# Field products of embeddings: embedding depth on the partitions, the batch along the free dimension, one fixed weight, all loads in the sync queue, and two tiles loaded ahead instead of three

## Chip, cores, metric

One core of one Trainium2 chip. The metric is device time in microseconds (us) for one execution; the host's preparation of arrays is not in it. A kernel's time is the median of its runs; a profile, and every number read from it, is of one execution; "1302" for the kernel before was measured again (medians 1301.9 to 1302.3 us).

## The reference

```python
def reference(r_x, L0_rec_W):            # x: (4096, 32, 64), W: (64, 64), fp32
    vid = jnp.einsum('bfd,de->bfe', x, W)
    idx_i, idx_j = jnp.triu_indices(32, k=1)        # 496 pairs of fields
    return x[:, idx_i, :] * vid[:, idx_j, :]        # (4096, 496, 64)
```

The output has 520 MB, the input 34 MB. All arithmetic is small beside the writing.

## The kernel before

Batch rows lie on the partitions. A tile is 128 rows with all 32 fields; two tiles share one load. W multiplies from the right, so each pair of fields is transposed by TensorE first, copied out of PSUM, multiplied, and copied again; VectorE then forms the pair products into one of three output buffers, and each buffer is stored on the sync queue. Mid-run loads go on the scalar queue, three loads ahead.

```python
    R = 2                       # tiles per load
    SLOT = 171                  # pairs (of 64 elements) in an output buffer
    AHEAD = 3                   # loads ahead, and x buffers
    ...
    def load(g):
        queue = nc.sync if g < AHEAD else nc.scalar
        xt = xpool.tile([P, R, F, D], F32, tag="x", name=f"x_{g}")
        ...                     # g == 0: in three pieces
            queue.dma_start(out=xt, in_=xg[g])
    ...
    def project(xt, r, tag, order):
        for g in order:         # four groups of four pairs of fields
            for k, pair in enumerate(pairs):
                nc.tensor.transpose(pt[:, k, :], xt[:, r, 2*pair : 2*pair+2, :], ident)
            nc.scalar.copy(xT[:, g*TPB : (g+1)*TPB, :], pt)
            for k, pair in enumerate(pairs):
                for h in range(2):
                    nc.tensor.matmul(pv[:, h, k, :], lhsT=xT[h*D:(h+1)*D, pair, :],
                                     rhs=w2[h*D:(h+1)*D, :], start=True, stop=True)
            nc.scalar.copy(vid[...], pv[:, :, :TPB, :])
    ...
            nc.vector.tensor_tensor(ot[...], xt[:, r, i:i+1, :].to_broadcast([P, n, D]),
                                    vid[:, i+1:, :], ALU.mult)
    ...                         # then one store of the buffer on nc.sync
```

Of the kernel before, what the change touches and what calls it, by code (L numbers as in the profile page):

```python
# [1 line left out]

# [5 lines left out]

F32 = mybir.dt.float32
ALU = mybir.AluOpType  # L10



SLOTS = [(0, 6), (6, 13), (13, 31)]

FIRST = [(13, 31, [24, 18, 13]), (6, 13, [10, 8, 6]), (0, 6, [4, 2, 0])]
SECOND = [(0, 6, [2, 4, 6]), (6, 13, [8, 10, 13]), (13, 31, [18, 31])]


@with_exitstack  # L20
def pairwise_bilinear_kernel(
    ctx: ExitStack,
    tc: tile.TileContext,
    x: bass.AP,
    w: bass.AP,
    out: bass.AP,
):
    nc = tc.nc
    P = 128
    B, F, D = x.shape  # L30
    NP = F * (F - 1) // 2

    R = 2
    G = B // (P * R)


    TPB = 4
    GRP = F // 2 // TPB
    SLOT = 171
    AHEAD = 3  # L40

    xg = x.rearrange("(g p r) f d -> g p r f d", p=P, r=R)
    og = out.rearrange("(g p r) n d -> g p r n d", p=P, r=R)
    off = [i * (F - 1) - i * (i - 1) // 2 for i in range(F)]

    const = ctx.enter_context(tc.tile_pool(name="const", bufs=1))
    xpool = ctx.enter_context(tc.tile_pool(name="x", bufs=AHEAD))
    tpool = ctx.enter_context(tc.tile_pool(name="xT", bufs=1))
    vpool = ctx.enter_context(tc.tile_pool(name="vid", bufs=2))
    opool = ctx.enter_context(tc.tile_pool(name="out", bufs=3))  # L50
    ps_t = ctx.enter_context(
        tc.tile_pool(name="ps_t", bufs=4, space=bass.MemoryType.PSUM)
    )
    ps_v = ctx.enter_context(
        tc.tile_pool(name="ps_v", bufs=2, space=bass.MemoryType.PSUM)
    )

    w2 = const.tile([P, D], F32)
    nc.scalar.dma_start(out=w2[0:D, :], in_=w)
    nc.scalar.dma_start(out=w2[D : 2 * D, :], in_=w)  # L60

    def load(g):
        queue = nc.sync if g < AHEAD else nc.scalar
        xt = xpool.tile([P, R, F, D], F32, tag="x", name=f"x_{g}")
        if g == 0:
            h = F // 2
            nc.sync.dma_start(out=xt[:, 0, h:, :], in_=xg[g][:, 0, h:, :])
            nc.sync.dma_start(out=xt[:, 0, :h, :], in_=xg[g][:, 0, :h, :])
            for r in range(1, R):
                nc.sync.dma_start(out=xt[:, r], in_=xg[g][:, r])  # L70
        else:
            queue.dma_start(out=xt, in_=xg[g])
        return xt

    loaded = [load(g) for g in range(AHEAD)]

    ident = const.tile([P, P], F32)
    make_identity(nc, ident)

    def project(xt, r, tag, order):  # L80

        xT = tpool.tile([P, F // 2, P], F32, tag="xT", name=f"xT_{tag}")
        vid = vpool.tile([P, F // 2, 2, D], F32, tag="vid", name=f"vid_{tag}")
        for g in order:
            pairs = range(g * TPB, (g + 1) * TPB)
            pt = ps_t.tile([P, TPB, P], F32, tag="pt", name=f"pt_{tag}_{g}")
            for k, pair in enumerate(pairs):
                nc.tensor.transpose(  # L88
                    pt[:, k, :], xt[:, r, 2 * pair : 2 * pair + 2, :], ident
                )  # L90
            nc.scalar.copy(xT[:, g * TPB : (g + 1) * TPB, :], pt)  # L91

            pv = ps_v.tile([P, 2, 2 * TPB, D], F32, tag="pv", name=f"pv_{tag}_{g}")
            for k, pair in enumerate(pairs):
                for h in range(2):
                    nc.tensor.matmul(  # L96
                        pv[:, h, k, :],
                        lhsT=xT[h * D : (h + 1) * D, pair, :],
                        rhs=w2[h * D : (h + 1) * D, :],
                        start=True,  # L100
                        stop=True,
                    )
            nc.scalar.copy(  # L103
                vid[:, g * TPB : (g + 1) * TPB].rearrange("p k h e -> p h k e"),
                pv[:, :, :TPB, :],
            )
        return vid.rearrange("p g h e -> p (g h) e")

    def products(xt, vid, ot, base, r, fields):
        for i in fields:  # L110
            n = F - 1 - i
            nc.vector.tensor_tensor(  # L112
                ot[:, off[i] - base : off[i] - base + n, :],
                xt[:, r, i : i + 1, :].to_broadcast([P, n, D]),
                vid[:, i + 1 :, :],
                ALU.mult,
            )

    for g in range(G):
        xt = loaded[g]  # L120
        for r in range(R):
            t = g * R + r
            first = t == 0
            vid = project(xt, r, t, range(GRP - 1, -1, -1) if first else range(GRP))
            plan = FIRST if first else SECOND if t == 1 else None
            for s, (lo, hi) in enumerate(SLOTS):
                if plan:
                    lo, hi, ends = plan[s]
                else:
                    ends = [hi]  # L130
                ot = opool.tile([P, SLOT, D], F32, tag="o", name=f"o_{t}_{s}")
                base = off[lo]
                at = hi if first else lo
                for e in ends:
                    a, b = (e, at) if first else (at, e)
                    products(xt, vid, ot, base, r, range(b - 1, a - 1, -1) if first else range(a, b))
                    nc.sync.dma_start(
                        out=og[g][:, r, off[a] : off[b], :],
                        in_=ot[:, off[a] - base : off[b] - base, :],
                    )  # L140
                    at = e
        if g + AHEAD < G:
            loaded.append(load(g + AHEAD))


_INS = ["r_x", "L0_rec_W"]
_OUTS = [((4096, 496, 64), "float32")]


# [21 lines left out]
```

## Time and profile before

| | before |
|---|---|
| time | 1301.97 us (1301.0 to 1302.68) |
| span of the profiled run | 1300.3 us |
| written, read | 520.09 MB, 33.59 MB |
| VectorE, TensorE, ScalarE busy | 87%, 26%, 10% of the span |
| share of 16 DMA engines, sync and scalar queue | 94.5% and 4.9% |

The page is to be read for what fills the span. The compute engines do not; the DMA queues do. What is left to find in such a kernel is where the sixteen DMA engines are *not* moving data, and that needs the rate by stretches of time. The prediction below shows those lines.

The last 26.8 us of the span show how evenly the engines run dry (columns: stretch, length, busy us of TensorE, its weight loads, VectorE, ScalarE, GpSimd with counts, granted TensorE clock, DMA share, GB/s). The kernel before:

```profile
1273.50:1300.30 26.80, 0.00 (x0) 0.00 (x0) 0.64 (x4) 0.00 (x0) 0.00 (x0) 0.50 0.69 296
```

Computing is over here but for 0.64 us and the stores are queued, yet the engines are busy for only 69% of the stretch: some have finished while others still have stores to do.

### The profile page before, as it was taken

The numbers are of one execution on the slowest core, as the hardware profiler recorded it, in microseconds if no ns is written. First come the engines' busy times: TensorE is split into PE (matmuls) and PEld (weight loads), VectorE is DVE, ScalarE is ACT, GpSimd is POOL, SyncE is SP. The second block draws the span as 40 slices with busy tenths as digits, with TensorE's granted clock in tenths as the row PEclk, the third lists the DMA queues.
The fourth block names the chain that finished last, engine by engine and source line by source line (L and its number), as shares of the span: only waits on it lengthen the run. The fifth ranks groups of instructions, "written<-read, shape, count | busy, mean of one in ns | idle before, by whom it ended". The sixth has DMA issues, their size and how long they took to land.

```text
span 1300.3 us, 6845 instructions
## 1 busy us (share of the span) xinstructions
PE 336.3 (26%) x2560; PEld 315.8 (24%) x2560; DVE 1132.8 (87%) x992; ACT 136.4 (10%) x257; POOL 0.7 (0%) x6
## 2 busy tenths in 40 slices
PE   7333213332033320333203332033330233321000
PEld 6333203332033320333203332033330223311000
DVE  6999979889798897988979899798987979999991
ACT  3111101111011110111101111001110011110000
POOL 0000000000000000000000000000000000000000
PEclk9555555555555555555555555555555555555555
DMA  9999999999999999999999999999999999999997
GB/s 384 430 421 439 428 430 436 423 432 430 428 429 430 434 422 436 435 422 433 433 429 431 423 434 424 430 435 428 433 426 427 437 421 430 434 433 431 436 431 318
DMA packets 18193, 554.12 MB, mean 426 GB/s; under 512 B 2160, under 2 KB 2160, under 8 KB 2544
## 3 DMA queue, kind: packets, MB, share of 16 engines
q1 hardware_dynamic: 16128, 526.39, 94.5%
q10 hardware_dynamic: 2032, 27.30, 4.9%
q8 instruction: 20, 0.33, 0.1%
q14 instruction: 13, 0.11, 0.0%
HBM read 33.59 MB, written 520.09 MB: 426 GB/s over the span
## 4 chain that ended last, share of the span: by engine, by line
DMA 62%; DVE 35%; issue 1%; PE 0%; DVEq 0%; ACT 0%
DMA out_dram<-o 61%; DVE o L112 35%; DMA x<-in_r_x_dram 0%; PE pt L88 0%; PE pv L96 0%; DVEq L166 0%; DVEq L112 0%; ACT vid L103 0%
## 5 line engine op out<-in xcount | busy, mean ns | idle before, releaser
L112 DVE TENSOR_TENSOR o<-x,vid 128x64 f32<-128x64 f32 (+30 forms) x992 | 1132.8, 1219 | 141.3 <-DMA out_dram<-o 130.2
L96 PE MATMUL pv<-w,xT 64*128 64x64 f32 x2048 | 230.0, 413 | 862.0 <-ACT vid L103 827.8
L96 PEld LDWEIGHTS pv<-w,xT 64*128 64x128 f32 x2048 | 218.2, 320 | 878.6 <-ACT vid L103 837.7
L103 ACT COPY vid<-pv 128x512 f32<-128x512 f32 x128 | 72.1, 587 | 1060.2 <-DVE o L112 971.3
L88 PE MATMUL pt<-ident,x 128*128 128x128 f32 x512 | 108.8, 397 | 5.4 <-DMA x<-in_r_x_dram 5.4
L88 PEld LDWEIGHTS pt<-ident,x 128*128 128x128 f32 x512 | 97.6, 212 | 9.0 <-issue 5.3
L91 ACT COPY xT<-pt 128x512 f32<-128x512 f32 x128 | 66.4, 610 | 5.7 <-PE pt L88 5.6
L91 ACT ACT_TABLE_LOAD x1 | 1.3, 1283 | 2.0 <-issue 2.0
masks.py:199 POOL TENSOR_SCALAR_AFFINE_SELECT ident<-ident 128x128 f32<-128x128 f32 x1 | 0.3, 292 | 0.1
masks.py:197 POOL MEMSET ident<- 128x128 f32 x1 | 0.2, 204 | 0.3 <-POOLq L157 0.3
L157 POOL MEMSET const-bfloat16-1.0<- 128x1 bf16 x1 | 0.1, 102 | 0.0
L157 POOL MEMSET const-uint8-127<- 128x1 uint8 x1 | 0.1, 102 | 0.0
L157 POOL MEMSET const-float32-0.0<- 128x1 f32 x1 | 0.1, 99 | 0.2 <-issue 0.2
L157 POOL MEMSET const-float32-1.0<- 128x1 f32 x1 | 0.1, 99 | 0.0
## 6 DMA issues: line engine op xcount, KB each, us to landing
out_dram<-o SPq DMA_DIRECT2D x60, 5472.0 KB, 25.5
out_dram<-o SPq DMA_DIRECT2D x30, 4928.0 KB, 28.4
x<-in_r_x_dram ACTq DMA_DIRECT2D x13, 2048.0 KB, 23.0
out_dram<-o SPq DMA_DIRECT2D x2, 2560.0 KB, 12.8
x<-in_r_x_dram SPq DMA_DIRECT2D x2, 2048.0 KB, 14.4
out_dram<-o SPq DMA_DIRECT2D x2, 1952.0 KB, 11.6
out_dram<-o SPq DMA_DIRECT2D x2, 1920.0 KB, 11.6
out_dram<-o SPq DMA_DIRECT2D x2, 1824.0 KB, 11.6
```

Source lines behind the costliest of these rows:

```text
L88: nc.tensor.transpose(pt[:, k, :], xt[:, r, 2 * pair : 2 * pair + 2, :], ident)
L91: nc.scalar.copy(xT[:, g * TPB : (g + 1) * TPB, :], pt)
L96: nc.tensor.matmul(pv[:, h, k, :], lhsT=xT[h * D : (h + 1) * D, pair, :], rhs=w2[h * D : (h + 1) * D, :], start=True, stop=True,)
L103: nc.scalar.copy(vid[:, g * TPB : (g + 1) * TPB].rearrange("p k h e -> p h k e"), pv[:, :, :TPB, :],)
L112: nc.vector.tensor_tensor(ot[:, off[i] - base : off[i] - base + n, :], xt[:, r, i : i + 1, :].to_broadcast([P, n, D]), vid[:, i + 1 :, :], ...
L157: nc = _bacc.Bacc("TRN2", target_bir_lowering=False, num_devices=1)
```

## The change

The host permutes x to (tile, 2 x 64 depth, field, 128 batch rows), so the depth that the product contracts is already on the partitions. W becomes the stationary operand of every matmul, and transposes, the identity and one of the two PSUM copies go. Instructions become twice as wide and fewer. The output is written in the same order and permuted back by the host. At the same time the loads move to the sync queue, in program order among the stores, and only two tiles are loaded ahead (4.2 MB instead of 6.3; the x tile is still 16 KB a partition).

Two words are used from here on. A *ring* is the part of a queue that one DMA engine works off. A *seam* is a load that stands among stores, with the change from stores to the load and back.

```diff
-    SLOT = 171
-    AHEAD = 3
+    SLOT = 83                     # pairs of 128 elements
+    AHEAD = 2
...
-        queue = nc.sync if g < AHEAD else nc.scalar
-        xt = xpool.tile([P, R, F, D], F32, tag="x", name=f"x_{g}")
+            xs[t] = xpool.tile([P, F, C], F32, tag="x", name=f"x_{t}")
+        nc.sync.dma_start(out=xs[t][:, lo:hi, :], in_=x[t][:, lo:hi, :])
...
-                nc.tensor.transpose(pt[:, k, :], xt[:, r, 2*pair : 2*pair+2, :], ident)
-            nc.scalar.copy(xT[:, g * TPB : (g + 1) * TPB, :], pt)
...
-                        pv[:, h, k, :],
-                        lhsT=xT[h * D : (h + 1) * D, pair, :],
-                        rhs=w2[h * D : (h + 1) * D, :],
+                        pv[half, b : b + BANK, :],
+                        lhsT=w2[half, :],
+                        rhs=xs[t][half, f : f + BANK, :],
...
+                store(t, ot, base, base, top)
+                if 1 <= n <= PIECES and t + 1 < NT and t + 1 not in (0, 1):
+                    load(t + 1, (n - 1) * F // PIECES, n * F // PIECES)
...
+    x = x.reshape(2, NT, C, F, D).transpose(1, 0, 4, 3, 2).reshape(NT, 2 * D, F, C)
```

More of the change, by code (lines that the diff above doesn't have):

```diff
@@ L5 @@
 from concourse import mybir
-from concourse.masks import make_identity
 from concourse._compat import with_exitstack
@@ L10 @@
 ALU = mybir.AluOpType
-SLOTS = [(0, 6), (6, 13), (13, 31)]
-FIRST = [(13, 31, [24, 18, 13]), (6, 13, [10, 8, 6]), (0, 6, [4, 2, 0])]
-SECOND = [(0, 6, [2, 4, 6]), (6, 13, [8, 10, 13]), (13, 31, [18, 31])]
+P = 128
+C = 128
 @with_exitstack
@@ L28, in pairwise_bilinear_kernel @@
     nc = tc.nc
-    P = 128
-    B, F, D = x.shape
+    NT, _, F, _ = x.shape
+    D = P // 2
     NP = F * (F - 1) // 2
-    R = 2
-    G = B // (P * R)
-    TPB = 4
-    GRP = F // 2 // TPB
-    SLOT = 171
-    AHEAD = 3
-    xg = x.rearrange("(g p r) f d -> g p r f d", p=P, r=R)
-    og = out.rearrange("(g p r) n d -> g p r n d", p=P, r=R)
+    GRP = 8
+    NGRP = F // GRP
+    BANK = 512 // C
+    SLOT = 83
+    AHEAD = 2
+    PIECES = 1
     off = [i * (F - 1) - i * (i - 1) // 2 for i in range(F)]
+    ctx.enter_context(tc.manual_schedule(engines={mybir.EngineType.SP}))
     const = ctx.enter_context(tc.tile_pool(name="const", bufs=1))
     xpool = ctx.enter_context(tc.tile_pool(name="x", bufs=AHEAD))
-    tpool = ctx.enter_context(tc.tile_pool(name="xT", bufs=1))
     vpool = ctx.enter_context(tc.tile_pool(name="vid", bufs=2))
     opool = ctx.enter_context(tc.tile_pool(name="out", bufs=3))
-    ps_t = ctx.enter_context(
-        tc.tile_pool(name="ps_t", bufs=4, space=bass.MemoryType.PSUM)
-    )
-    ps_v = ctx.enter_context(
-        tc.tile_pool(name="ps_v", bufs=2, space=bass.MemoryType.PSUM)
+    psum = ctx.enter_context(
+        tc.tile_pool(name="ps", bufs=4, space=bass.MemoryType.PSUM)
     )
@@ L60, in pairwise_bilinear_kernel, with load, project @@
     nc.scalar.dma_start(out=w2[D : 2 * D, :], in_=w)
-    def load(g):
-        queue = nc.sync if g < AHEAD else nc.scalar
-        xt = xpool.tile([P, R, F, D], F32, tag="x", name=f"x_{g}")
-        if g == 0:
-            h = F // 2
-            nc.sync.dma_start(out=xt[:, 0, h:, :], in_=xg[g][:, 0, h:, :])
-            nc.sync.dma_start(out=xt[:, 0, :h, :], in_=xg[g][:, 0, :h, :])
-            for r in range(1, R):
-                nc.sync.dma_start(out=xt[:, r], in_=xg[g][:, r])
-        else:
-            queue.dma_start(out=xt, in_=xg[g])
-        return xt
-    loaded = [load(g) for g in range(AHEAD)]
-    ident = const.tile([P, P], F32)
-    make_identity(nc, ident)
-    def project(xt, r, tag, order):
-        xT = tpool.tile([P, F // 2, P], F32, tag="xT", name=f"xT_{tag}")
-        vid = vpool.tile([P, F // 2, 2, D], F32, tag="vid", name=f"vid_{tag}")
-        for g in order:
-            pairs = range(g * TPB, (g + 1) * TPB)
-            pt = ps_t.tile([P, TPB, P], F32, tag="pt", name=f"pt_{tag}_{g}")
-            for k, pair in enumerate(pairs):
-                nc.tensor.transpose(
-                    pt[:, k, :], xt[:, r, 2 * pair : 2 * pair + 2, :], ident
-                )
-            nc.scalar.copy(xT[:, g * TPB : (g + 1) * TPB, :], pt)
-            pv = ps_v.tile([P, 2, 2 * TPB, D], F32, tag="pv", name=f"pv_{tag}_{g}")
-            for k, pair in enumerate(pairs):
+    xs = {}
+    def load(t, lo, hi):
+        if t not in xs:
+            xs[t] = xpool.tile([P, F, C], F32, tag="x", name=f"x_{t}")
+        nc.sync.dma_start(out=xs[t][:, lo:hi, :], in_=x[t][:, lo:hi, :])
+    def project(t, order):
+        vid = vpool.tile([P, F, C], F32, tag="vid", name=f"vid_{t}")
+        for g in order:
+            pv = psum.tile([P, GRP, C], F32, tag="pv", name=f"pv_{t}_{g}")
+            for b in range(0, GRP, BANK):
+                f = g * GRP + b
                 for h in range(2):
+                    half = slice(h * D, (h + 1) * D)
                     nc.tensor.matmul(
-                        pv[:, h, k, :],
-                        lhsT=xT[h * D : (h + 1) * D, pair, :],
-                        rhs=w2[h * D : (h + 1) * D, :],
+                        pv[half, b : b + BANK, :],
+                        lhsT=w2[half, :],
+                        rhs=xs[t][half, f : f + BANK, :],
                         start=True,
@@ L102, in project, with products @@
                     )
-            nc.scalar.copy(
-                vid[:, g * TPB : (g + 1) * TPB].rearrange("p k h e -> p h k e"),
-                pv[:, :, :TPB, :],
-            )
-        return vid.rearrange("p g h e -> p (g h) e")
-    def products(xt, vid, ot, base, r, fields):
-        for i in fields:
-            n = F - 1 - i
+            nc.scalar.copy(vid[:, g * GRP : (g + 1) * GRP, :], pv)
+        return vid
+    def products(t, vid, ot, base, a, b, backwards=False):
+        fields = [i for i in range(F - 1) if off[i] < b and off[i + 1] > a]
+        for i in reversed(fields) if backwards else fields:
+            s, e = max(a, off[i]), min(b, off[i + 1])
+            j = i + 1 + s - off[i]
@@ L112, in products @@
             nc.vector.tensor_tensor(
-                ot[:, off[i] - base : off[i] - base + n, :],
-                xt[:, r, i : i + 1, :].to_broadcast([P, n, D]),
-                vid[:, i + 1 :, :],
+                ot[:, s - base : e - base, :],
+                xs[t][:, i : i + 1, :].to_broadcast([P, e - s, C]),
+                vid[:, j : j + e - s, :],
                 ALU.mult,
             )
-    for g in range(G):
-        xt = loaded[g]
-        for r in range(R):
-            t = g * R + r
-            first = t == 0
-            vid = project(xt, r, t, range(GRP - 1, -1, -1) if first else range(GRP))
-            plan = FIRST if first else SECOND if t == 1 else None
-            for s, (lo, hi) in enumerate(SLOTS):
-                if plan:
-                    lo, hi, ends = plan[s]
-                else:
-                    ends = [hi]
-                ot = opool.tile([P, SLOT, D], F32, tag="o", name=f"o_{t}_{s}")
-                base = off[lo]
-                at = hi if first else lo
-                for e in ends:
-                    a, b = (e, at) if first else (at, e)
-                    products(xt, vid, ot, base, r, range(b - 1, a - 1, -1) if first else range(a, b))
-                    nc.sync.dma_start(
-                        out=og[g][:, r, off[a] : off[b], :],
-                        in_=ot[:, off[a] - base : off[b] - base, :],
-                    )
-                    at = e
-        if g + AHEAD < G:
-            loaded.append(load(g + AHEAD))
@@ new lines, in store @@
+    def store(t, ot, base, a, b):
+        nc.sync.dma_start(out=out[t][:, a:b, :], in_=ot[:, a - base : b - base, :])
+    for g in reversed(range(NGRP)):
+        load(0, g * GRP, (g + 1) * GRP)
+    load(1, F // 2, F)
+    load(1, 0, F // 2)
+    for t in range(NT):
+        vid = project(t, reversed(range(NGRP)) if t == 0 else range(NGRP))
+        bases = list(range(0, NP, SLOT))
+        if t == 0:
+            ends = [NP, off[27], off[24], off[21], bases[-1]]
+            for n, base in enumerate(reversed(bases)):
+                top = min(base + SLOT, NP)
+                if n:
+                    ends = [top, (base + top) // 2, base]
+                ot = opool.tile([P, SLOT, C], F32, tag="o", name=f"o_{t}_{n}")
+                for b, a in zip(ends, ends[1:]):
+                    products(t, vid, ot, base, a, b, backwards=True)
+                    store(t, ot, base, a, b)
+        else:
+            for n, base in enumerate(bases):
+                top = min(base + SLOT, NP)
+                ot = opool.tile([P, SLOT, C], F32, tag="o", name=f"o_{t}_{n}")
+                products(t, vid, ot, base, base, top)
+                store(t, ot, base, base, top)
+                if 1 <= n <= PIECES and t + 1 < NT and t + 1 not in (0, 1):
+                    load(t + 1, (n - 1) * F // PIECES, n * F // PIECES)
@@ L157 @@
     nc = _bacc.Bacc("TRN2", target_bir_lowering=False, num_devices=1)
+    x = _np.asarray(inputs["r_x"])
+    B, F, D = x.shape
+    NT = B // (2 * C)
+    x = x.reshape(2, NT, C, F, D).transpose(1, 0, 4, 3, 2).reshape(NT, 2 * D, F, C)
     arrays, args = {}, []
-    for name in _INS:
-        a = _np.ascontiguousarray(inputs[name])
+    for name, a in zip(_INS, (x, inputs["L0_rec_W"])):
+        a = _np.ascontiguousarray(a)
         arrays[f"in_{name}_dram"] = a
@@ L164 @@
         dt = _mybir.dt.from_np(_np.dtype(dtype))
-        args.append(nc.dram_tensor(f"out_{i}_dram", shape, dt, kind="ExternalOutput").ap())
+        laid = (NT, 2 * D, shape[1], C)
+        args.append(nc.dram_tensor(f"out_{i}_dram", laid, dt, kind="ExternalOutput").ap())
     with _tile.TileContext(nc) as tc:
@@ L168 @@
     r = _run(nc, [arrays], core_ids=[0])
-    got = tuple(r.results[0][f"out_{i}_dram"] for i in range(len(_OUTS)))
-    return got[0]
+    got = r.results[0]["out_0_dram"].reshape(NT, 2, D, _OUTS[0][0][1], C)
+    return _np.ascontiguousarray(got.transpose(1, 0, 4, 3, 2)).reshape(_OUTS[0][0])
```

## The prediction

> **What bounds the kernel now.** I read the page from the top: busy shares, then the slices and queues, then the chain that ended last; after that the windows view for the two ends of the run, where a transfer-bound kernel can still differ.
>
> ```profile
> span 1300.3 us, 6845 instructions
> PE 336.3 (26%) x2560; PEld 315.8 (24%) x2560; DVE 1132.8 (87%) x992; ACT 136.4 (10%) x257; POOL 0.7 (0%) x6
> ...
> q1 hardware_dynamic: 16128, 526.39, 94.5%
> q10 hardware_dynamic: 2032, 27.30, 4.9%
> q8 instruction: 20, 0.33, 0.1%
> ...
> HBM read 33.59 MB, written 520.09 MB: 426 GB/s over the span
> DMA 62%; DVE 35%; issue 1%; PE 0%; DVEq 0%; ACT 0%
> ```
>
> The reader should see two things. TensorE and ScalarE, which the change relieves, are busy for 26% and 10%. The packets of the queues fill 94.5 + 4.9 = 99.4% of the sixteen DMA engines' span. VectorE's 35% of the chain misleads: it alternates with the stores because each of the three output buffers is filled, stored and filled again. The waits settle it: VectorE's 130 us of waiting are nearly all for output stores to land, and while it works on one buffer, the stores of the two others are queued. So **the store and load traffic is the bound**, from a few us after the start to the end. The windows view says where it falls short of full rate (columns: stretch, length, busy of each engine with counts, granted TensorE clock, DMA share, GB/s):
>
> ```profile
> 0.00:3.00 3.00, 0.00 (x0) 0.00 (x0) 0.00 (x0) 1.03 (x1) 0.70 (x6) 1.00 0.34 94
> 3.00:6.00 3.00, 0.64 (x3) 0.67 (x4) 0.00 (x0) 0.25 (x1) 0.00 (x0) 1.00 0.97 341
> 6.00:15.00 9.00, 9.00 (x67) 8.55 (x66) 3.85 (x10) 3.96 (x7) 0.00 (x0) 1.00 1.03 438
> 15.00:20.00 5.00, 4.85 (x50) 4.21 (x50) 5.00 (x6) 2.41 (x6) 0.00 (x0) 1.00 0.98 372
> ...
> 100.00:1280.00 1180.00, 291.71 (x2176) 274.33 (x2176) 1043.97 (x920) 115.71 (x220) 0.00 (x0) 0.53 1.00 430
> 1280.00:1300.30 20.30, 0.00 (x0) 0.00 (x0) 0.00 (x0) 0.00 (x0) 0.00 (x0) 0.50 0.58 252
> ```
>
> The time can be put together from this. 554.12 MB at the 430 GB/s of the middle is 1288.7 us. The start loses 3 x (1 - 94/430) + 3 x (1 - 341/430) + 5 x (1 - 372/430) = 2.3 + 0.6 + 0.7 = 3.6 us. The last stretch loses 20.3 x (1 - 252/430) = 8.4 us. Sum 1300.7 against 1300.3 measured. The 8.4 us is not VectorE: its last product ends at 1274 us. The sixteen engines run dry at different times. The landing times of the last store, one per engine in the trace, lie 10.4 us apart, against 1.2 to 1.4 us for the first two; the gap grows in steps, mostly while a load is in flight.
>
> **What the Trainium skill says.** *DMA: Bandwidth & Descriptors*, Specifications, gives 435 GB/s as the fabric ceiling and about 358 GB/s as the share of a core in HBM. The trace agrees with the first (430 in the middle) and not with the second as a limit for a core that runs alone. The same page, Issuing engines are not separate DMA queues, says that transfers started by sync or scalar run on the same 16 engines; the trace agrees, since q1 and q10 sum to 99.4%. So moving the loads to the sync queue adds no bandwidth. *VectorE: DVE Perf Modes*, The TRN2 errata, gives (N+151)/0.96 ns for an fp32 tensor_tensor; for N = 1984 that is 2224 ns, and the trace has 2225. *Runtime: NRT & Kernel Launch*, Instruction fetch mechanics, says that instructions are fetched by DMA in blocks of 16 KiB, 256 instructions. The trace agrees: 5120 TensorE records / 256 = 20, the packet count of q8.
>
> **The change part by part.**
>
> ```profile
> L112 DVE TENSOR_TENSOR o<-x,vid 128x64 f32<-128x64 f32 (+30 forms) x992 | 1132.8, 1219 | 141.3 <-DMA out_dram<-o 130.2
> L96 PE MATMUL pv<-w,xT 64*128 64x64 f32 x2048 | 230.0, 413 | 862.0 <-ACT vid L103 827.8
> L88 PE MATMUL pt<-ident,x 128*128 128x128 f32 x512 | 108.8, 397 | 5.4 <-DMA x<-in_r_x_dram 5.4
> L91 ACT COPY xT<-pt 128x512 f32<-128x512 f32 x128 | 66.4, 610 | 5.7 <-PE pt L88 5.6
> ```
>
> *Traffic.* Unchanged. x is still 16 KB contiguous per partition and tile, out about 42.5 KB contiguous per partition and store (83 pairs x 128 x 4 bytes, before 43.8 and 39.4), with the same 248 KiB between partitions. The host's permutes are not in the device time. Only fetches shrink: TensorE goes from 2560 to 512 matmul records (256 fp32 matmuls, two records each, as 1024 made 2048 before), saving 16 of the 20 q8 packets, 0.26 MB. Base: 553.8 / 430 = 1287.9 us.
>
> *Removed, off the path.* 512 transposes (108.8 us) and 128 copies (66.4 us) go. Both engines idle for most of the run, so outside the start this is worth 0.
>
> *VectorE.* Same elements per partition, 32 x 31,744 = 1.016 M. The slope between the 64 and the 1984 rows (219 and 2225 ns) is 1.045 ns per element; back to back, an instruction adds about 75 ns. 581 instead of 992 instructions: 1061 + 581 x 0.075 = 1105 us, 28 us less. This is slack, not time: a store slot costs VectorE about 11.6 us and the DMA 12.6.
>
> *TensorE in mid-run.* 32 records of 64 columns took 3.68 us at a granted clock of 0.5, so 115 ns each; 512 columns make 920 ns and a tile's 32 records 29 us if the two half-arrays do not overlap. A load is issued behind two stores and lands some 31 us after its issue; VectorE wants the new vid some 56 us after it. So vid may be 3 us late (31 + 29), with 25 us of stores still queued. Hidden.
>
> *The start, the one place on the path.* Before, the first product starts at 11.15 us, the first store is issued at 13.6, and three loads (6.3 MB) keep the engines busy until about 17: no gap. After, only two tiles (4.2 MB) are loaded ahead, enough until about 12.6 us. The first chunk lands at the same time (5.4 us). The first group is 8 records of 512 columns: 7.5 us at the rate of the early burst (16 of 64 columns in 1.93 us), half that if the halves overlap or the clock rises. A copy twice as wide takes 1.1 us. First product at 10.3 to 14, say 12. Then the first stores carry 10, 18, 27 and 26 pairs, ready 1.7, 4.4, 8.2 and 11.9 us later, while the DMA needs 1.6, 2.8, 4.1 and 4.0 us for them, plus about 1.3 us from issue to data. Gaps: 2.4 + 1.1 + 1.1 + 0 + 1.5 (before the fifth) = **6 us** (4.4 to 8). The 3.6 us stay: 9.6 in all.
>
> *The loads.* While a load runs beside stores, single store packets take up to 2.3 us instead of 1.6; over all engines I count some 0.6 us per load, 8 us in all, already inside the 430. One ring keeps the mixing to the two seams of each load; the same seam at 15 to 20 us cost 0.7 us in one ring. I take 2 us off, with 0 to 6 possible.
>
> *The tail.* Fewer fetches, less interleaving: I take 5.5 for 8.4 us, and this is a choice.
>
> Sum: 1287.9 + 9.6 - 2 + 5.5 = 1301 us of span. The run's own time lies 1.7 us above the span (1302.08 and 1300.3). That makes 1302.7; because two of the terms can only shrink I go a little lower, **1299 us**.
>
> **The rivals.** (1) *The single ring heals the loads*: no slow packets (-6 us), engines end within 3 us of one another (tail 4 us). For it: the gap grows during loads on the second queue. Against it: the seam at 15 us. Time about 1292. (2) *The start costs more or the seams are worse*: a FIFO load holds the stores behind it, TensorE stays at half clock without overlap. Time about 1308. (3) *VectorE or TensorE becomes the bound*, through a late vid or the two x buffers. Against it: 1105 us of VectorE work against 1288 of transfers, and 10 us of spare queue; a further 2% would need a stall of 26 us. (4) *The removed 175 us of transposes and copies come back as time.* Against it: ScalarE's and TensorE's share of the chain is 0%.
>
> **Range and chances.** The moving terms (start 4 us, seams 4, tail 4, about independent) give some 7 us each way, widened for an unseen change in the rate: 1290 to 1309. Faster by 2% would need under 1276, below 553.8 MB at the best 433 GB/s seen, so 1%. Slower by 2% needs 26 us that I see nowhere: 2%.
>
> **What would show it right or wrong.** Right: DMA still fills over 97% of the engines' span at 428 to 433 GB/s in the middle; a dip between 12 and 31 us; VectorE near 1105 us and waiting on stores; TensorE under 480 us, all hidden; q8 down to about 4 packets and q10 to the weights alone. The step on seams is wrong if the middle runs above 432 or below 427; that on the tail if the last 20 us lose over 9 or under 4 us; that on the start if the first 40 us lose under 6 or over 13. The whole is wrong if VectorE stops waiting for stores in mid-run, which would mean a new bound, or if the rate of stores differs with the new layout.

## The result

The changed kernel took **1310.42 us** (1308.58 to 1310.78, four runs) against 1301.97. The ratio is 1.0063, 95% interval 1.0045 to 1.0080. A ratio here is the mean time of one kernel's runs over that of the other's runs of the same rounds, so it is not quite the ratio of the medians. The kernel is 8.4 us slower, and 1.4 us beyond the upper end of the predicted range.

The page of the changed kernel, in the parts that answer to those of before:

```profile
span 1306.8 us, 2101 instructions
PE 146.9 (11%) x512; PEld 45.9 (4%) x512; DVE 1105.8 (85%) x581; ACT 66.1 (5%) x65; POOL 0.2 (0%) x4
...
q1 hardware_dynamic: 17856, 553.66, 98.9%
q8 instruction: 4, 0.07, 0.0%
...
HBM read 33.59 MB, written 520.09 MB: 424 GB/s over the span
...
L88 DVE TENSOR_TENSOR o<-x,vid 128x1408 f32<-128x1408 f32 (+15 forms) x581 | 1105.8, 1974 | 174.6 <-DMA out_dram<-o 162.8
L72 PE MATMUL pv<-x,w 64*64 64x512 f32 x512 | 146.9, 730 | 1043.4 <-DMA x<-in_r_x_dram 1038.2
```

Everything that was removed is gone: TensorE's busy time fell by 189 us and VectorE's by 27 us, and VectorE waits more than before (174.6 us), still for stores. There is one full queue instead of two, and the whole rate is 424 GB/s instead of 426. So the bound is the same and it is used a little worse. The windows view says where:

```profile
12.00:15.00 3.00, 3.00 (x16) 0.95 (x14) 3.00 (x6) 1.50 (x2) 0.00 (x0) 1.00 0.56 234
15.00:20.00 5.00, 5.00 (x26) 1.61 (x24) 5.00 (x6) 2.89 (x4) 0.00 (x0) 1.00 0.77 317
20.00:30.00 10.00, 3.05 (x14) 0.70 (x10) 10.00 (x8) 2.69 (x3) 0.00 (x0) 0.74 0.82 347
...
100.00:1200.00 1100.00, 129.12 (x448) 40.90 (x448) 942.99 (x491) 56.68 (x56) 0.00 (x0) 0.56 1.00 430
...
1280.00:1306.80 26.80, 0.00 (x0) 0.00 (x0) 0.41 (x2) 0.00 (x0) 0.00 (x0) 0.50 0.58 252
```

The middle runs at 430 GB/s, as before. Two ends are worse. Between 12 and 30 us the engines are busy for 56 to 82% only: VectorE works without a pause and cannot yet fill the stores. By the formula of the prediction the first 30 us lose 7.8 us, against 3.6 before. And the last 26.8 us lose 26.8 x (1 - 252/430) = 11.1 us, against 26.8 x (1 - 296/430) = 8.4 us.

### The profile page after: what moved, and what is told of

Read it like the earlier page. It is cut to its first block, busy times and chain, and to the rows that moved or that the text cites. A ratio compares the mean times of both kernels' runs of the same rounds, so it can differ in the third digit from the quotient of the medians.

```text
span 1306.8 us, 2101 instructions
## 1 busy us (share of the span) xinstructions
PE 146.9 (11%) x512; PEld 45.9 (4%) x512; DVE 1105.8 (85%) x581; ACT 66.1 (5%) x65; POOL 0.2 (0%) x4
## 4 chain that ended last, share of the span: by engine, by line
DMA 63%; DVE 31%; issue 3%; PE 0%; DVEq 0%; ACT 0%
DMA out_dram<-o 63%; DVE o L88 31%; PE pv L72 0%; DMA w<-in_L_rec_W_dram 0%; DVEq L154 0%; ACT vid L79 0%; DVEq L88 0%
## 5 line engine op out<-in xcount | busy, mean ns | idle before, releaser
L88 DVE TENSOR_TENSOR o<-x,vid 128x1408 f32<-128x1408 f32 (+15 forms) x581 | 1105.8, 1974 | 174.6 <-DMA out_dram<-o 162.8
L72 PE MATMUL pv<-x,w 64*64 64x512 f32 x512 | 146.9, 730 | 1043.4 <-DMA x<-in_r_x_dram 1038.2
L79 ACT COPY vid<-pv 128x1024 f32<-128x1024 f32 x64 | 64.8, 1012 | 1123.4 <-PE pv L72 1123.4
L72 PEld LDWEIGHTS pv<-x,w 64*64 64x64 f32 x512 | 45.9, 165 | 1143.5 <-issue 1130.3
```

The source lines that it names most:

```text
L72: nc.tensor.matmul(pv[half, b : b + BANK, :], lhsT=w2[half, :], rhs=xs[t][half, f : f + BANK, :], start=True, stop=True,)
L79: nc.scalar.copy(vid[:, g * GRP : (g + 1) * GRP, :], pv)
L88: nc.vector.tensor_tensor(ot[:, s - base : e - base, :], xs[t][:, i : i + 1, :].to_broadcast([P, e - s, C]), vid[:, j : j + e - s, :], ALU ...
```

## The experiments

**Theory.** Three things add up. G: two tiles ahead leave a gap at the start. S: loads in line with the stores let one DMA engine fall behind the others, and the last engine sets the end. L: the layout by itself is no slower. **Rivals.** R: engines fall behind with loads in any queue, and just as far. N: the new layout's stores, or a seam of its own, cost time. All times are in this table; the last column comes from the trace's packet records. Packets of one DMA engine follow each other without a gap (typically a packet starts within 5 ns of the end of another), so they can be joined into sixteen chains, and the column says how far the last chain's end lies behind the mean of the sixteen. It stands on one profiled execution for each kernel, and e3_ahead3_act and e3_again, the same kernel, differ by 1.4 us in it; a smaller difference says nothing.

| run | median us (range) | ratio to before [95%] | last engine behind mean, us |
|---|---|---|---|
| before | 1302 | 1 | 6.4 |
| changed | 1310.42 (1308.58-1310.78) | 1.0063 [1.0045, 1.0080] | 9.4 |
| e1_ahead3 | 1302.60 (1300.17-1305.55) | 1.0007 [0.9993, 1.0020] | 8.7 |
| e2_actload | 1305.38 (1304.60-1305.89) | 1.0026 [1.0014, 1.0039] | 6.1 |
| e3_ahead3_act | 1298.18 (1296.30-1299.95) | 0.9971 [0.9959, 0.9984] | 6.2 |
| e4_noload (wrong on purpose) | 1226.61 (1226.05-1226.72) | 0.9421 [0.9406, 0.9435] | 1.0 |
| e5_before_sync | 1302.76 (1302.26-1303.00) | 1.0005 [0.9992, 1.0017] | 8.6 |
| e6_pieces2 | 1319.38 (1318.34-1320.27) | 1.0133 [1.0119, 1.0147] | 9.9 |
| e7_slot62 | 1300.04 (1298.38-1302.41) | 0.9984 [0.9970, 0.9997] | 5.8 |
| e8_pairs | 1296.82 (1295.90-1297.87) | 0.9960 [0.9947, 0.9972] | 4.0 |
| e3_again | 1298.69 (1296.28-1300.95) | 0.9972 [0.9959, 0.9984] | 7.6 |
| e10_fetch | 1302.53 (1301.09-1302.97) | 1.0001 [0.9989, 1.0014] | 8.4 |
| e9_pairs_act | 1300.39 (1298.17-1301.35) | 0.9985 [0.9971, 0.9998] | 5.3 |
| e11_before_ahead2 | 1307.94 (1306.79-1308.64) | 1.0044 [1.0031, 1.0058] | 6.1 |

### The start: three tiles ahead

```diff
-    AHEAD = 2
+    AHEAD = 3
     load(1, 0, F // 2)
+    load(2, 0, F)
...                               # in mid-run: load(t + 2, ...) instead of load(t + 1, ...)
```

> The changed kernel with three x tiles loaded ahead instead of two, the third as one 2 MB load at the start, as the kernel before has it. Theory G (the gap between 12 and 30 us is on the path): the rate stays near 430 GB/s from 6 us on, the first 30 us lose some 4 us as in the kernel before instead of 7.9, and the time falls by 3 to 5 us from 1310.4, to about 1306. Rival (the gap is made up later by slack): under 1.5 us of change. The tail, which the third tile should not touch, stays at 10 to 12 us lost.

It fell by 7.8 us, about twice as much as G had said. The gap is closed (windows view of this run):

```profile
12.00:15.00 3.00, 3.00 (x17) 1.22 (x14) 3.00 (x5) 2.02 (x2) 0.00 (x0) 1.00 1.05 445
15.00:20.00 5.00, 5.00 (x26) 2.86 (x24) 5.00 (x5) 3.04 (x3) 0.00 (x0) 1.00 0.99 400
20.00:30.00 10.00, 9.16 (x42) 4.76 (x38) 10.00 (x8) 2.02 (x2) 0.00 (x0) 1.00 1.02 431
...
1274.30:1301.10 26.80, 0.00 (x0) 0.00 (x0) 0.44 (x2) 0.00 (x0) 0.00 (x0) 0.50 0.61 263
```

VectorE's first products are no earlier. It is the third load that keeps the engines busy while VectorE gets ahead. The windows account for 4.3 us of it. The two profiled executions are only 5.7 us apart (1308.58 us, the fastest of the changed kernel, and 1302.88), and of the rest 0.7 is the smaller lag of the last engine; one load fewer in mid-run is worth about 1 us (below). The other 2 us of the 7.8 lie between the profile and the median of the changed kernel and can't be placed in a trace. The tail stayed bad (263 GB/s), as expected.

The old layout confirms that it is the depth and not the layout:

```diff
-    AHEAD = 3
+    AHEAD = 2                     # in the kernel before, nothing else
```

> The kernel before with two x buffers instead of three, so 4.2 MB loaded ahead instead of 6.3 and nothing else changed. If the depth of the first loads is what costs in the changed kernel, the old layout shows it as well: a dip between 12 and 26 us and 5 to 8 us more, 1307 to 1310 us. If the gap belongs to the wider copies and matmuls of the new layout, within 2 us of 1302.

It took 1307.94 us, 5.7 more than before, inside G's range. The same hole opens (windows view):

```profile
12.00:15.00 3.00, 3.00 (x24) 2.88 (x23) 3.00 (x7) 1.75 (x3) 0.00 (x0) 1.00 0.51 216
15.00:20.00 5.00, 4.85 (x50) 4.21 (x48) 5.00 (x6) 2.20 (x5) 0.00 (x0) 1.00 0.54 223
```

### The queue: mid-run loads back on the scalar queue

```diff
-        nc.sync.dma_start(out=xs[t][:, lo:hi, :], in_=x[t][:, lo:hi, :])
+        queue = nc.sync if t < AHEAD else nc.scalar
+        queue.dma_start(out=xs[t][:, lo:hi, :], in_=x[t][:, lo:hi, :])
```

> The changed kernel with only its mid-run loads put back on the scalar queue. Theory S (loads in line with the stores make one engine fall behind at each of the 14 loads, 11.6 us in the end): the last store lands over 7 to 10 us instead of 11.6, the last 27 us lose about 8 us instead of 11.1, time down 2 to 4 us to about 1307. Rival R (engines fall behind with any load beside stores, whatever the queue): the tail stays at 10 to 12 us and the time within 1.5 us of 1310.4. The start gap stays in both.

It took 5.0 us less than the changed kernel, more than S had said. The tail, in the same view as above:

```profile
1276.90:1303.70 26.80, 0.00 (x0) 0.00 (x0) 0.47 (x2) 0.00 (x0) 0.00 (x0) 0.50 0.70 303
```

303 GB/s instead of 252, or 3.2 us less lost: the whole difference of the two profiled spans (1303.7 and 1306.8 us), and some two thirds of the 5.0 between the medians. The last engine is 6.1 us behind the mean instead of 9.4, while the mean end of the sixteen is the same in both profiles (1296.3 and 1296.2 us). R falls in its claim that the queue makes no difference. But engines do part with loads in either queue: 6.1 us are left here, against 1.0 without mid-run loads (e4_noload, below).

### Both edits

> Both edits at once: three tiles ahead and mid-run loads on the scalar queue. If G and S are both right and add up, it lands at the kernel before, 1301 to 1304 us. If only G holds, about 1306; if something of the new layout itself costs time (rate of stores, VectorE), it stays above 1305 although start and tail look like before.

1298.18 us, and 1298.69 when it was run again as a control. The queue is worth 4.4 us beside e1_ahead3 on the same chip; the third tile is worth 7.2 us beside e2_actload. The two add. The tail of the first profile is again that of the kernel before, that of the repeat is worse:

```profile
1270.30:1297.10 26.80, 0.00 (x0) 0.00 (x0) 0.42 (x2) 0.00 (x0) 0.00 (x0) 0.50 0.69 296
...
1271.30:1298.10 26.80, 0.00 (x0) 0.00 (x0) 0.40 (x2) 0.00 (x0) 0.00 (x0) 0.50 0.65 279
```

Here the queue moves more than the last engine: against e1_ahead3 the mean of the sixteen ends 1.6 and 1.9 us earlier in the two profiles, and the lag is 2.4 and 1.1 us smaller.

And it lands 3.7 us *below* the kernel before, which nobody had expected: with start and queue as before, the new layout alone is a gain of 0.29%, with its interval clear of 1. So N falls as an account of the 8.4 us; whether the ring costs time in the new layout alone is another question (e5_before_sync, below).

### No loads in mid-run

```diff
-                    load(t + 1, (n - 1) * F // PIECES, n * F // PIECES)
+                    xs[t + 1] = xs[t - 1]        # wrong result on purpose
```

> The changed kernel without the 14 mid-run loads: every later tile reads the first two x tiles again, so the result is wrong on purpose. It leaves 524.5 MB. If the loads alone make the engines part (theory S or R), the last store lands over less than 3 us, the middle runs at 433 GB/s, and the time is about 1210 + 8 + 3 + 2 = 1222 us, 88 us less than with the loads, although their bytes at 430 GB/s are only 68 us. If the engines part for another reason (unequal engines, fetches), the tail still loses about 11 us at 430 GB/s and the time is about 1240.

```profile
100.00:400.00 300.00, 36.30 (x128) 10.35 (x128) 282.39 (x148) 15.04 (x16) 0.00 (x0) 0.56 1.00 431
...
1198.00:1224.80 26.80, 0.00 (x0) 0.00 (x0) 0.48 (x2) 0.00 (x0) 0.00 (x0) 0.50 0.89 382
```

1226.6 us: 83.8 us less for 29.4 MB, which at 430 GB/s are 68.3 us. Fourteen loads thus cost 15.5 us beyond their bytes. Without them the engines stay together to the end (382 GB/s in the last stretch; the last store lands over 1.4 us instead of 11.6). It is the loads that part them. The middle came out at 431 to 432 GB/s, not 433, and the time 4 us above the expectation, whose terms sum to 1223 and not 1222.

### Twice the seams, half the seams

```diff
-    PIECES = 1
+    PIECES = 2                    # each load in two halves, behind two stores
```

> The changed kernel with each mid-run load cut into two halves, behind the second and the third store of a tile: 28 seams between stores and loads instead of 14, same bytes. If a seam costs a fixed time (the 14 loads cost 15 us more than their bytes at 430 GB/s), 5 to 15 us slower than 1310.4. If the cost goes with the bytes read beside writes, the same within 2 us.

9.0 us slower for 14 more seams, 0.64 us each, at the same bytes. The packets of a load are halved too, but that is not it: two of 8 KB take 2 x 309 ns where one of 16 KB takes 611, which is 0.8 us over the run. The middle shows the loss:

```profile
100.00:1200.00 1100.00, 159.19 (x432) 47.20 (x432) 936.18 (x486) 54.65 (x54) 0.00 (x0) 0.56 1.00 425
```

The other way round needs smaller output buffers, to have room for two tiles in one transfer. So there is a control with the small buffers:

```diff
-    SLOT = 83                     # control: 62, and four x tiles ahead
-    AHEAD = 2
+    SLOT = 62
+    AHEAD = 4
```

> A control: the changed kernel with output buffers of 62 pairs instead of 83 and four x tiles ahead (both needed for the next run), 12 mid-run loads, one by one in the sync queue. Like the run with three ahead, the start gap should be closed: about 1302 us. Two fewer loads in mid-run may take 1 us off[...].

and the kernel with pairs:

```diff
+    def load_pair(t, queue):
+        both = xpool.tile([P, 2, F, C], F32, tag="x", name=f"x_{t}")
+        xs[t], xs[t + 1] = both[:, 0], both[:, 1]
+        queue.dma_start(out=both, in_=x[t : t + 2].rearrange("t p f c -> p t f c"))
...
+                if n == 1 and t % 2 == 0 and t + 2 < NT:
+                    load_pair(t + 2, nc.sync)
```

> As the control, but mid-run loads of two tiles in one transfer: 6 of 4 MB instead of 12 of 2 MB, still in the sync queue. If the cost sits at the seams, about half of it goes: 3 to 6 us below the control, and the last store lands over about half the spread. If it goes with the bytes, the same as the control within 1.5 us, and an engine that is behind falls back twice as far per load.

The control took 1300.04 us and the pairs 1296.82: 3.2 us less for 6 seams fewer, 0.54 us each, and the fastest kernel, 0.40% below the kernel before (0.9960, interval 0.9947 to 0.9972). The spread did not halve; the last store landed over 5.8 us instead of 7.1. Both directions agree on something over half a microsecond for each seam saved or added. The cost is not quite fixed: by the packets (next section) an engine loses 0.76 us around a single load of the control and 1.02 around a double one.

### What a seam does to an engine

This is read from the chains of packets of the changed kernel. The typical store packet takes 1571 ns and the typical load packet 611 ns, again and again to the nanosecond. Around each load, single packets take up to 1 or 2 us longer. Over the 14 loads this costs an engine 0.57 us per load on average. But the engine that was furthest behind *before* the load (counted from three packets before it to six after it) loses 1.17 us, the others 0.53, and more than the others at 13 of the 14 loads (e1_ahead3: 1.16 and 0.61, 10 of 13). One load after another, 14 x (1.17 - 0.57) = 8.4 us of lag would grow out of this, and the table has 9.4.

Accordingly the first load packets of the sixteen engines start over 0.7 us at the first such load and over 12.1 us at the last. On the scalar queue they start over 0.6 to 2.5 us at every load of e2_actload: that queue is empty when a load is issued, so an engine that is behind with its stores reads at the same time as the others. The mean loss per load is about the same there (0.66 us). In this pair of profiles the queue changes who bears the loss. That a late engine suffers *because* it reads while the others write is my reading of this pattern; no run tried it alone.

### Only the queue, in the old layout: a miss

```diff
-        queue = nc.sync if g < AHEAD else nc.scalar
+        queue = nc.sync
```

> The kernel before with its mid-run loads on the sync queue, nothing else changed. Theory S (loads in line with the stores cost 4 to 5 us, as the two pairs of the last runs showed for the new layout): 1305 to 1307 us, the last store landing over 11 to 13 us instead of 10.4. Rival N (the cost belongs to the new layout, whose stores and loads have other sizes and seams): within 1.5 us of 1301.9.

1302.76 us, within 0.6 us of the kernel before (ratio 1.0005, interval with 1 in it): in the time, N was right and S wrong. In the profile the last engine lags all the same:

```profile
1274.40:1301.20 26.80, 0.00 (x0) 0.00 (x0) 1.23 (x5) 0.00 (x0) 0.00 (x0) 0.50 0.60 261
```

The tail falls from 296 to 261 GB/s, the last engine goes from 6.4 to 8.6 us behind the mean. The first load packets of the sixteen engines start over 1.2 us at the first mid-run load and over up to 9.8 at later ones. But the mean end comes 1.3 us earlier (431 to 433 GB/s from 100 us on instead of 430, though 419 instead of 429 between 30 and 100 us), so the sum is nearly nil. And the pattern of the section before is hardly there: the engine furthest behind loses 0.40 us around a load, the others 0.45 (0.56 and 0.45 with ten packets counted on each side). So that pattern is no general rule of one ring; where this lag comes from, and why the mean end comes earlier, stays open.

### The fetches

```diff
+        dm = psum1.tile([P, D], F32, tag="dm", name=f"dm_{t}")
+        for _ in range(64):
+            nc.tensor.matmul(dm[0:D, :], lhsT=w2[0:D, :], rhs=xs[t][0:D, 0, 0:D],
+                             start=True, stop=True)      # in e3_ahead3_act; results unused
```

> The control with 64 more small matmuls a tile, whose results nobody reads, so that TensorE has as many instruction records (5120) and fetches (20 blocks of 16 KiB) as the kernel before; one PSUM buffer fewer. Theory F (the control beats the kernel before by 3.7 us because of 16 fewer fetches, which stretch single engines): 1300 to 1302 us. Rival: the added 0.26 MB are 0.6 us, the rest of the 3.7 us comes from elsewhere: at most 1 us slower than the control.

Its page shows that the instruction count and the fetches of the kernel before are restored, and VectorE untouched:

```profile
PE 290.1 (22%) x2560; PEld 172.8 (13%) x2560; DVE 1105.7 (85%) x581; ACT 63.4 (5%) x65; POOL 0.2 (0%) x4
...
q8 instruction: 20, 0.33, 0.1%
```

1302.53 us, 3.8 us above the control of the same set, intervals apart. F did better than its rival: the edit that brings 16 fetches of 16 KiB takes back the whole advantage of the new layout, six times their 0.6 us of bytes. The packets show a part of it. Each fetch in mid-run takes 0.88 to 0.97 us, where a load packet of the same size takes 0.61, and the next store packet on the same DMA engine takes some 0.4 us longer: 1.3 us of one engine for each fetch, 21 us for 16, or 1.3 us of time if they fell evenly on the sixteen engines. The other 2.5 us need engines that part (the tail below has 265 GB/s against 279 and 296 of the two controls) or another cause:

```profile
1274.40:1301.20 26.80, 0.00 (x0) 0.00 (x0) 0.40 (x2) 0.00 (x0) 0.00 (x0) 0.50 0.61 265
```

The run also makes TensorE busier and has a PSUM buffer less. TensorE remains idle for most of the time and VectorE's busy time is the same, so the fetches are the likely cause, but only the fetches and these two together were tried: this is not shown.

### Pairs on the scalar queue: a miss

```diff
-                    load_pair(t + 2, nc.sync)
+                    load_pair(t + 2, nc.scalar)
```

> The kernel with buffers of 62 pairs and loads of two tiles (1296.8 us with all loads in the sync queue), with the 6 mid-run loads on the scalar queue. If what the queue is worth adds to what fewer seams are worth, another 2 to 4 us: 1293 to 1295 us, the fastest of all. If fewer seams had already removed what the queue removes, the same as 1296.8.

1300.39 us. What the queue is worth for 13 or 14 single loads is not there for 6 double ones; here the sync queue looks better (ratios 0.9985 and 0.9960 to the kernel before, intervals just touching at 0.9971 and 0.9972). By the packets an engine loses 1.37 us around a double load instead of 1.02, 2.1 us over the six; the last engine is 5.3 us behind instead of 4.0. I have no explanation that a run has tested.

## Why the prediction was wrong

**Right.** The bound and its rate (430 GB/s in the middle, forecast 428 to 433); VectorE at 1105.8 us (1105) and waiting on stores; first product at 11.83 us (12); the dip between 12 and 30 us; four fetch packets on q8 and all of TensorE hidden. That class, within 2%, was left 97%. TensorE was hidden by more than forecast: 9.2 us busy a tile (146.9 / 16) where the prediction had 29, so its worry about a vid 3 us late (its numbers give 31 + 29 - 56 = 4) was empty. The first group of TensorE took 5.5 us, where the prediction had 7.5 without overlap (its rate gives 7.7).

**The step that failed: the loads.** "One ring keeps the mixing to the two seams of each load ... I take 2 us off, with 0 to 6 possible." The sign was wrong: the ring cost 4.4 us (e1_ahead3 against e3_ahead3_act) to 5.0 us (changed against e2_actload), 6.4 to 7 us away from the estimate. The loss per load was sized well (0.6 us forecast, 0.57 measured), but one ring did not lower it. The prediction had seen that the gap between the engines grows while a load is in flight, and in its first rival put it down to the second queue. The runs show the reverse in this layout: with the second queue all engines take the load within 2.5 us of one another, and in one ring each comes to it when its own stores are done, 12.1 us apart at the end, and the last engine loses twice what the others lose. That swapping the queue costs these 4.4 to 5.0 us is shown by two pairs of runs; that the lag is how, is read from the packets, and e5_before_sync, with the lag and no loss of time, says that it is not the whole of it.

The sign that the prediction had set for this step, a middle above 432 or below 427 GB/s, did not show: the middle ran at 430. The loss sat at the end. The sign for the tail did: the last 20 us lose 11.4 us (185 GB/s), over its limit of 9.

**The tail** depended on the same mistake. "Fewer fetches, less interleaving: I take 5.5 for 8.4 us." With one ring it became 11.1 us. "Less interleaving" made it worse. What fewer fetches are worth in the tail alone can't be told: e3_ahead3_act has the tail of before (296 GB/s in both) and is 3.7 us faster, its repeat has 279 GB/s, and e10_fetch, which gives the 3.7 us back, 265.

**The start** was about right in the profile (7.8 us lost in the first 30 us, forecast 9.6) but is worth 7.2 to 7.8 us in time, where the sum had 6, "4.4 to 8".

**The last choice.** "Because two of the terms can only shrink I go a little lower" took another 3.7 us off, from 1302.7 to 1299, for no measured reason. Both the loads and the tail grew.

| term | predicted, us | measured, us |
|---|---|---|
| start, two tiles ahead | +6 (4.4 to 8) | +7.2 and +7.8 |
| loads in one ring | -2 (0 to -6) | +4.4 and +5.0 |
| the rest: bytes of fetches and tail | -3.7 | -3.7 (e3_ahead3_act against before) |

The measured terms must sum to about the 8.4 us, since both ways from the kernel before to the changed one lead over e3_ahead3_act; what they show is that the two effects add to within 0.6 us. That the third row agrees is luck: it was to come from the tail (2.9) and the bytes of the fetches (0.8), and is what the whole layout is worth once start and queue are as before. The second rival ("about 1308", a start that costs more or seams that are worse) was the nearest. Of its reasons the worse seams came true; the start that costs more did in the medians, by 1 to 2 us, and the half clock did not: it was 1.00 until 20 us.

**Still open:** some 2 us of the start, how much of the ring's cost is the lag of the last engine, why the old layout doesn't pay for one ring, why pairs don't gain from two, and what of the 3.7 us is the fetches.

## What to carry to other kernels

When a kernel is bound by transfers, count the time in which any DMA engine is without work: at the start until the first stores flow, at each change between loads and stores, and at the end by the slowest engine. Load deep enough at the start to cover the first computing, make mid-run loads few and large (6 double loads for 12 saved 3.2 us here), and compare both queues on the chip rather than argue for one: here the better one differed with the layout and the size of a load. Emptying compute engines off the path was worth at most 3.7 us here, probably by the fetches it saved, and the settings that travel with it (here a prefetch depth and a queue) can cost more than it brings.

## What the Trainium skill lacked or had wrong

- *DMA: Bandwidth & Descriptors*, Issuing engines are not separate DMA queues, says that starting transfers on several engines only saves the sequencer's time to initiate them. Here the queue of 13 or 14 loads of 2 MB made 4.4 to 5.0 us of 1300 in one layout, with the last DMA engine 8.7 to 9.4 us behind the mean in one ring and 6.1 to 7.6 with two; in the other layout it made no difference clear of noise (0.6 us), with a lag of 8.6 and 6.4.
- No page that I read gives a cost for a load between stores in mid-stream. 14 loads of 2 MB cost 15.5 us beyond their bytes; 14 more seams cost 9.0 us, 6 fewer saved 3.2 us.
- *Runtime: NRT & Kernel Launch*, Instruction fetch mechanics, calls the crossing of a 16 KiB boundary "mostly hidden". Here each fetch in mid-run held one DMA engine for 0.88 to 0.97 us and the store packet behind it some 0.4 us longer, and the edit that brought 16 more of them to this transfer-bound kernel cost 3.8 us.
- *DMA: Bandwidth & Descriptors*, Where 436 GB/s comes from, says in one sentence that for transfers between HBM and SBUF the HBM side (about 358 GB/s) binds. For a core that runs alone this is wrong, as the 425 GB/s that the same paragraph calls near fabric rate suggests: all kernels here ran at 423 to 433 GB/s in the middle, on one core.
